# Attention in a chain of four layers: every fourth addition of exp by an adding transfer, sums in exp's own tiles, compact inversion of the softmax sums, single PSUM banks

## The chip, the cores and the metric

The kernel runs on one core of a Trainium2 chip. The metric is the device time of one execution in microseconds; the median of several runs counts. A profiled execution is one further run, of which every instruction of each engine is recorded: TensorE (PE; its weight loads are listed apart as PEld), VectorE (DVE), ScalarE (ACT), GpSimd (POOL) and the queue engine SyncE (SP), with the DMA transfers that SP, ACT and POOL issue.

## The reference

The input `x` has 16 frames of 384 channels and 16 by 16 points. Two sequences of 8 frames each make 2048 tokens. Four layers follow; the change concerns the first, attention with 12 heads of 32 channels, whose values are the input itself:

```python
xt = x.reshape(B, NUM_FRAMES, C, H, W).transpose(0, 2, 1, 3, 4)
xt = xt.reshape(B, C, N).transpose(0, 2, 1)
qk = (xt @ qk_w.T).reshape(B, N, 2, nh, HEAD_DIM)
...
v = xt.reshape(B, N, nh, HEAD_DIM).transpose(0, 2, 1, 3)
attn = jax.nn.softmax(jnp.einsum('bhnd,bhmd->bhnm', q * scale, k), axis=-1)
attn = alpha * eye + beta * attn - gamma * Cm
out = jnp.einsum('bhnm,bhmd->bhnd', attn, v)
```

`Cm` is constant (1/N). Layer 1 is a 7 by 7 depthwise convolution, a layer norm, a gelu network with a response norm and a residual; layer 2 a Sobel edge pair, a product, a layer norm and gelu; layer 3 two small products with a 3 by 3 depthwise convolution, linear attention, a layer norm and a gelu network. All is float32.

## The kernel before

**Attention** (`attention`, from L399). Channels stand on partitions, tokens along the columns; 512 tokens are a block (`BLK`), 128 a key tile. A unit is one sequence and one group of four heads (`units`, six of them); a unit has four query blocks, so 24 blocks in all, and each block has 16 steps `t`, one for each key tile: 384 steps.

A step is two halves. `scores(n, t)` makes four products `st` (one for each head, 32 channels deep, so that the four run in different rows of the PE) into two PSUM tiles of two banks each, and two exps of 1024 columns on ACT into the SBUF tiles `e`. `weighted(n, t, es)` of the step before comes after it: four products `av` (each with 32 result rows) that add e times v into one PSUM bank over all 16 steps, and the additions of `e` on DVE. The softmax needs the sum over all keys; the kernel adds the `e` of several steps on DVE into a tile `s`, and then the PE multiplies `s` with ones into the bank `dn`, which sums over partitions and spreads the sum over the 32 rows of a head. How many steps are added before such a product is in `ADDS`, one number of 16, 8, 4 or 2 for each of the 24 blocks: a small number is less adding on DVE and more products on the PE. The products of one group are put out in four quarters of 128 columns over the following steps (`weights`, through the table `due`, which holds what is to be issued at which step); a block's last group goes in one piece of 512.

At a block's end ACT copies `av` to `va`, makes `xg` (alpha times x plus the constant part), and `finish` copies `dn` to `r`. DVE inverts `r` in four pieces of 128 columns, one for each of four steps, then comes `va` times `r` and `l` (beta times that plus `xg`). ACT reads `r` once more for a bound that a check at the end looks at.

The PSUM has eight banks: three pairs for `st` (pool `pst`), one bank for `av` and one for `dn` (pool `pacc`). The q and k of later blocks are made by `project` at step 5 of a block (`SLOT`), two products at a time into one pair of banks; SP loads `v`.

PE, ACT and DVE run in the order in which the code issues (class `InOrder`). The order of everything else around attention is set by a planner: `Plan` keeps, for each engine, when it would be free, and for each pool how much room there is; each operation has a length, things it comes after, and what it takes and gives. `fill` is called in every step of attention, and `pace(t)` is its entry for the PE's and DVE's time in a step; what DVE has left goes to layer 1's convolution (`convolutions`, from step `FIRST`), which has only two `y` buffers during attention (`YB`), and from step `LEAD` to the first normalisations of layer 1 (`leads`). After attention `plan.all` orders layers 1 to 3 by the ranks in `RANK`, with `SLACK`, and `TURNS` gives the order in which blocks use the loaded weights of the two gelu networks.

Attention starts once the first x block and weights are there; the tail is almost only products of 128 by 128 by 512.

Of the kernel before, what the change touches and what calls it, by code (L numbers as in the profile page):

```python
# [13 lines left out]
PSUM = bass.MemoryType.PSUM  # L14

P = 128
# [15 lines left out]
SLOT = 5  # L32
LEAD = 20 * NQC + 6
# [3 lines left out]
    (0, ((0, 0), (0, 1), (0, 2), (0, 3),)),  # L37
    (1, ((0, 0), (0, 1),)),
    (0, ((1, 0), (1, 2),)),
    (1, ((0, 2),)),  # L40
    (0, ((1, 1), (1, 3),)),
    (1, ((1, 0), (0, 3), (1, 2), (1, 1), (1, 3),)),
# [4 lines left out]
    "mid": ((36.6, 22.0, 24.3, 85.6), (18.6, 42.9, 96.6, 26.9)),  # L47
    "l1": ((50.1, 89.5, 75.2, 4.0), (51.1, 16.8, 81.7, 28.5)),
    "l3c": ((45.7, 99.2, 100.9, 121.0), (-20.9, -6.3, 70.9, 62.0)),
    "conv": 109.4,  # L50
}
SLACK = 0.196
JUNK = 2

ADDS = (16, 8, 16, 16, 4, 4, 4, 2, 2, 8, 16, 16, 4, 16, 2, 4, 16, 8, 4, 4, 4, 4, 4, 4)
# [61 lines left out]
class Plan:  # L117
# [24 lines left out]
    def run(self, op):  # L142
        at = self.start(op)
        assert at is not None
        for tag, n in op.takes:
            del self.room[tag][:n]
        if op.engine == "PE" and at - self.free_at["PE"] > 2:
            at += 1.5
        if op.engine:
            self.free_at[op.engine] = at + op.length  # L150
        op.ready = at + op.length + op.lag
        for tag, n in op.gives:
            self.room[tag] = sorted(self.room[tag] + [op.ready] * n)
        if op.makes:
            self.made[op.makes] = op
        self.table = op.table or self.table
# [37 lines left out]
def pace(t):  # L194
# [3 lines left out]
    adds = ADDS[n]  # L198
    pe, dve = 2.066, 2.275 if t and i % adds else 0.0
    at = i - adds - 1  # L200
    parts = sum(j * adds // 4 == at % adds for j in range(4)) if at >= 0 else 0
    if parts:
        pe += 0.22 * parts
    elif i == 1 and n > 0:
        pe += 0.87
    else:
        pe += 0.09
    if n > 0:
        dve += {2: 0.88, 3: 0.88, 4: 0.88, 5: 0.88, 6: 0.6, 7: 0.66}.get(i, 0.0)
# [188 lines left out]
def attention(tc, X, xt, L0, block, small, col, cols, ones, load_qk, banks, fill, bound):  # L398
# [6 lines left out]
    with ExitStack() as actx:  # L405
# [3 lines left out]
        ep = pool("ep", 8)  # L409
        sp = pool("sp", 4)  # L410
        op = pool("op", 2)
        pst = pool("pst", 3, space=PSUM)
        pacc = pool("pacc", 1, space=PSUM)

        def bank2(name):
            return pst.tile([P, 2, BLK], F32, tag="st", name=name)

        banks.append(lambda name: bank2(name)[:, 0, :])
# [35 lines left out]
        due = {}  # L454

        def unit(u, made, gm):
# [3 lines left out]
            adds = ADDS[u * NBLK : (u + 1) * NBLK]  # L460
            acc, sums = {}, {}

            def scores(n, t):
                es = []
                for i in range(2):
                    es.append(ep.tile([P, 2, BLK], F32, tag="e", name=f"e_{u}_{n}_{t}_{i}"))
                sts = [bank2(f"st_{u}_{n}_{t}_{i}") for i in range(2)]
                for h in range(4):
                    rows = slice(HD * h, HD * (h + 1))
                    pe.matmul(  # L470
                        sts[h // 2][:, h % 2, :],
# [5 lines left out]
                for i in range(2):  # L477
                    act.activation(es[i], sts[i], AF.Exp, scale=HD**-0.5)
                return es

            def weighted(n, t, es):
                if t == 0:
                    acc["av"] = pacc.tile([P, BLK], F32, tag="av", name=f"av_{u}_{n}")
                for h in range(4):
# [3 lines left out]
                        es[h // 2][:, h % 2, :],  # L488
# [3 lines left out]
                at = t % adds[n]  # L492
                for i in range(2):
                    if at == 0:
                        sums[i] = es[i]
                    elif at == 1:
                        s = sp.tile([P, 2, BLK], F32, tag="s", name=f"s_{u}_{n}_{t}_{i}")
                        dve.tensor_tensor(s, sums[i], es[i], ALU.add)
                        sums[i] = s
                    else:  # L500
                        dve.tensor_tensor(sums[i], sums[i], es[i], ALU.add)


                k = (u * NBLK + n) * NQC + t
                if at == adds[n] - 1:
                    parts = 1 if t == NQC - 1 else 4
                    for i in range(parts):
                        due.setdefault(k + 2 + i * adds[n] // 4, []).append(
                            lambda i=i, summed=dict(sums): weights(
                                n, t, summed, ts(i, BLK // parts)  # L510
                            )
                        )
                for f in due.pop(k, ()):
                    f()
                if t == NQC - 1:
# [6 lines left out]
                    due[k + 2].append(lambda: finish(n, va, xg))  # L522

            def weights(n, t, summed, at):
                if t == adds[n] - 1 and at.start == 0:
                    acc["dn"] = pacc.tile([P, BLK], F32, tag="dn", name=f"dn_{u}_{n}")
                for h in range(4):
# [3 lines left out]
                        summed[h // 2][:, h % 2, at],  # L531
                        start=(t == adds[n] - 1 and at.start == 0),
# [3 lines left out]
            def finish(n, va, xg):  # L536
# [4 lines left out]
                r = op.tile([P, BLK], F32, tag="r", name=f"r_{u}_{n}")  # L541
                act.activation(r, acc["dn"], AF.Identity, accum_out=bound[:, 0, k : k + 1])

                def invert(i):
                    dve.reciprocal(r[:, ts(i, P)], r[:, ts(i, P)])
# [3 lines left out]

                def check():  # L550
# [1101 lines left out]
```

## Time and profile before

| what | value |
|---|---|
| runs | 2679.3 us median of 3 (2674.36 to 2680.14) |
| the profiled execution's own time | 2679.38 us |
| its span, first to last instruction | 2677.6 us |
| mean granted TensorE clock | 0.996 |
| attention, first `st` to first `ph` of layer 1 | 22.1 to 1052.3 us |
| PE busy in it | 1021.9 of 1030.2 us |
| DVE, ACT busy in it | 962.7 and 837.4 us |
| 96 reciprocals of r, 128x128 | 88.7 us, 939 ns each |
| `dn` products of 128 columns, of 512 | 84.3 us, 26.7 us |
| DMA issued by SP | 53 MB in all, mean 21 GB/s over the span |

In the profile, a group line gives the engine, the operation, `out<-in` by tile names, the form and the count, then the busy time in us, the mean of one in ns, the idle time of the engine just before, and what ended most of that idle time. L96 is the helper that issues in order, so groups are told apart by tile names. A window line gives a stretch in us, its length, then busy us and count of PE, PEld, DVE, ACT and POOL, the granted clock, the DMA share and GB/s. A timeline line gives the start in us, the length, the engine and what ran, with the idle time before it and its releaser in brackets. A DMA line gives count, size of one and median us from issue to landing.

### The profile page before, as it was taken

Reading aid. Unit: us, or ns where it says so; the run is one execution under the profiler, and the core shown is the slowest. Engines: PE = TensorE matmul, PEld = TensorE weight load, DVE = VectorE, ACT = ScalarE, POOL = GpSimd, SP = SyncE. Lnnn points to the kernel's source line nnn. Section 1 sums busy time; section 2 is a strip of 40 time slices with the busy share of each in tenths; the row PEclk is TensorE's granted clock in tenths of the full one; section 3 lists DMA queues with packets and bytes.
Section 4 is the critical chain, followed back from the end, with each engine's and each line's share of the span. In section 5 each row is a group of like instructions: output and inputs, shape, how many; then the busy total and the mean of one; then the engine's idle time right before and its main releaser. Section 6 shows DMA issues by size and latency. Waiting matters only on the chain. (4 is left out here: it accounts for less than half of the span.)

```text
span 2677.6 us, 32803 instructions
## 1 busy us (share of the span) xinstructions
PE 2644.6 (99%) x12997; PEld 1061.5 (40%) x12997; DVE 2011.5 (75%) x2588; ACT 1557.5 (58%) x2314; POOL 7.4 (0%) x54
## 2 busy tenths in 40 slices
PE   8999999999999999899999999999999999999999
PEld 2223333233323323345444454444444444454443
DVE  5999999999999889999999999999652202732300
ACT  6787878878787888564565335457443542625201
POOL 0000000000000000000000000000000000000000
PEclk9999999999999999999999999999999999999999
DMA  3000000000000003000001001011001110000000
GB/s 150 5 13 1 9 9 5 13 1 5 13 1 1 1 13 108 23 0 0 1 1 47 25 12 31 29 36 36 24 24 36 47 36 24 0 1 1 12 17 20
DMA packets 28851, 55.69 MB, mean 21 GB/s; under 512 B 1680, under 2 KB 14096, under 8 KB 28688
## 3 DMA queue, kind: packets, MB, share of 16 engines
q1 hardware_dynamic: 28544, 53.35, 6.0%
q8 instruction: 104, 1.70, 0.3%
q14 instruction: 59, 0.48, 0.1%
q10 hardware_dynamic: 144, 0.15, 0.0%
HBM read 47.21 MB, written 6.29 MB: 20 GB/s over the span
## 5 line engine op out<-in xcount | busy, mean ns | idle before, releaser
L96 ACT ACTIVATE e<-st 128x1024 f32<-128x1024 f32 x768 | 743.2, 1025 | 88.5 <-PE st L96 80.7
L96 DVE SCALAR_TENSOR_TENSOR y<-l,vec,y 128x420 f32<-128x420 f32 (+8 forms) x1152 | 660.0, 638 | 5.0
L96 DVE TENSOR_TENSOR s<-s,e 128x1024 f32<-128x1024 f32 x444 | 513.3, 1216 | 11.7 <-ACT e L96 11.2
L96 PE MATMUL st<-q,k 32*128 32x512 f32 x3072 | 474.1, 641 | 4.0 <-ACT e L96 2.3
L96 PE MATMUL av<-e,v 128*32 128x512 f32 x3072 | 410.9, 606 | 4.3 <-ACT va L96 4.2
L96 PE MATMUL ph_l<-y,wa 128*128 128x512 f32 x576 | 261.4, 597 | 0.0
L96 PE MATMUL ph_l3c<-d_l3c,wa 128*128 128x512 f32 x576 | 258.4, 593 | 0.0
L96 PE MATMUL po_l<-hid_l,wb 128*128 128x512 f32 x576 | 255.7, 596 | 1.1 <-ACT hid_l L96 1.1
L96 PE MATMUL po_l3c<-hid_l3c,wb 128*128 128x512 f32 x576 | 256.6, 593 | 0.0
L96 PEld LDWEIGHTS st<-q,k 32*128 32x128 f32 x3072 | 146.1, 183 | 220.1 <-issue 132.4
L96 DVE TENSOR_TENSOR s<-e,e 128x1024 f32<-128x1024 f32 x162 | 191.0, 1221 | 54.7 <-ACT e L96 36.0
L96 ACT ACTIVATE hid_l<-ph_l,vec 128x512 f32<-128x512 f32 x96 | 66.0, 687 | 202.9 <-PE ph_l L96 202.8
L96 ACT ACTIVATE hid_l3c<-ph_l3c,vec 128x512 f32<-128x512 f32 x96 | 65.6, 687 | 202.6 <-PE ph_l3c L96 202.5
L96 PEld LDWEIGHTS av<-e,v 128*32 128x32 f32 x3072 | 60.6, 108 | 298.1 <-issue 274.0
L96 DVE SCALAR_TENSOR_TENSOR o_l3c<-po_l3c,vec,l 128x512 f32<-128x512 f32 x24 | 17.5, 748 | 209.6 <-PE po_l3c L96 208.8
L96 PEld LDWEIGHTS po_l<-hid_l,wb 128*128 128x128 f32 x576 | 109.5, 191 | 139.1 <-issue 128.0
L96 PEld LDWEIGHTS ph_l3c<-d_l3c,wa 128*128 128x128 f32 x576 | 108.8, 190 | 137.2 <-issue 133.4
L96 PEld LDWEIGHTS ph_l<-y,wa 128*128 128x128 f32 x576 | 109.1, 191 | 136.0 <-issue 125.1
L96 PEld LDWEIGHTS po_l3c<-hid_l3c,wb 128*128 128x128 f32 x576 | 109.0, 190 | 134.6 <-issue 132.8
L96 PE MATMUL p<-x,wqk_sb 128*128 128x512 f32 x288 | 132.3, 610 | 1.2 <-DMA x<-in_x_dram 1.2
L96 DVE SCALAR_TENSOR_TENSOR g_l3a<-h_l3a,dw,g_l3a 128x450 f32<-128x450 f32 (+1 forms) x192 | 119.0, 702 | 4.2 <-ACT g_l3a L96 4.1
L96 PEld LDWEIGHTS dn<-s,ones 128*32 128x32 f32 x2016 | 64.1, 110 | 125.4 <-issue 107.0
(155 smaller groups left out, 2446.3 us busy)
## 6 DMA issues: line engine op xcount, KB each, us to landing
wa<-in_w_dram SPq DMA_DIRECT2D x9, 768.0 KB, 4.5
wb<-in_w_dram SPq DMA_DIRECT2D x9, 768.0 KB, 5.0
wa<-in_mlp_w_dram SPq DMA_DIRECT2D x9, 768.0 KB, 4.4
wb<-in_mlp_w_dram SPq DMA_DIRECT2D x9, 768.0 KB, 4.5
x<-in_x_dram SPq DMA_DIRECT2D x8, 768.0 KB, 10.6
v<-in_xt_dram SPq DMA_DIRECT2D x24, 256.0 KB, 2.7
out_dram<-o_l3c SPq DMA_DIRECT2D x24, 256.0 KB, 2.1
qkv<-in_qkv_wT_dram SPq DMA_DIRECT2D x3, 576.0 KB, 11.1
```

The source lines that it names most:

```text
L96: self.last = self.tc.keep_in_program_order(make(*args, **kw))
```

## The change

- `ADDS` goes. Every block has four groups of four steps. In a group, the second step's `e` is added to the first's by a DMA issued from POOL with `accum_op=ADD`; the fourth's is added to the third's by DVE, in place; then DVE adds the two results (`both`). The sums thus stand in `e`'s tiles, and the pool `sp` goes.
- `e` is one tile of 4 by 512 columns for a step; there are six of these where there were eight of 2 by 512 and four `s` of 2 by 512. Exp is issued for each head, 512 columns at a time.
- All eight PSUM banks are one pool of single banks, from which `st`, `av`, `dn` and the projections take.
- The quarters of `dn` come one step later; what would fall into the next block is, except for the last three blocks (`PAIRED`), collected in `late` and issued in that block's step 0, behind the projections, which move from step 5 to step 0.
- For the inversion, ACT copies `dn` to `sums`; one row of each head goes to DRAM (`away`), and comes back spread over 128 partitions of 16 columns (`few`). DVE inverts that, and it goes to DRAM (`back`) and back in four transfers that spread it over each head's 32 rows (`r`). ACT's bound reads `few`.
- `LEAD` is 24 times 16, past the last step. `pace` has new entries. The planner lets the weights' room be given back by a count of uses (`spent`). `TURNS`, `RANK` and `SLACK` have new values.

```diff
-        ep = pool("ep", 8)
-        sp = pool("sp", 4)
+        ep = pool("ep", 6)
...
-        pst = pool("pst", 3, space=PSUM)
-        pacc = pool("pacc", 1, space=PSUM)
...
+        pb = pool("pb", 8, space=PSUM, reuse_waits="tile")
+        dp = pool("dp", 2, space=DRAM)
...
-                for i in range(2):
-                    act.activation(es[i], sts[i], AF.Exp, scale=HD**-0.5)
+                for h in range(4):
+                    act.activation(es[:, h, :], sts[h], AF.Exp, scale=HD**-0.5)
...
+                if at % 2 == 0:
+                    acc[at] = es
+                elif at == 1:
+                    nc.gpsimd.dma_start(acc[0], es, accum_op=ALU.add)
+                else:
+                    dve.tensor_tensor(acc[2], acc[2], es, ALU.add)
+
+                    def both(summed=acc[0], other=acc[2]):
+                        dve.tensor_tensor(summed, summed, other, ALU.add)
+
+                    if end and block < PAIRED:
+                        late.append(both)
                     else:
...
+                        due.setdefault(k + 1, []).append(both)
+                    for i in range(1 if end else 4):
+                        f = lambda i=i, summed=acc[0]: weights(
+                            n, t, summed, ts(i, BLK if end else BLK // 4)
                         )
+                        when = k + 3 + i
+                        if block < PAIRED and when >= (block + 1) * NQC:
+                            late.append(f)
+                        else:
+                            due.setdefault(when, []).append(f)
...
-                r = op.tile([P, BLK], F32, tag="r", name=f"r_{u}_{n}")
-                act.activation(r, acc["dn"], AF.Identity, accum_out=bound[:, 0, k : k + 1])
-
-                def invert(i):
-                    dve.reciprocal(r[:, ts(i, P)], r[:, ts(i, P)])
+                sums = op.tile([P, BLK], F32, tag="sums", name=f"sums_{u}_{n}", bufs=1)
+                act.activation(sums, acc["dn"], AF.Identity, accum_out=bound[:, 0, k : k + 1])
+                away = dp.tile([4, BLK], F32, tag="away", name=f"away_{u}_{n}")
+                nc.sync.dma_start(away, sums[0:P:HD, :])
+                few = op.tile([P, BLK // HD], F32, tag="few", name=f"few_{u}_{n}")
+                nc.sync.dma_start(few, away.rearrange("h (j k) -> (h j) k", j=HD))
+                r = op.tile([P, BLK], F32, tag="r", name=f"r_{u}_{n}", bufs=1)
+
+                def invert():
+                    dve.reciprocal(few, few)
+                    back = dp.tile([P, BLK // HD], F32, tag="back", name=f"back_{u}_{n}")
+                    nc.sync.dma_start(back, few)
+                    for h in range(4):
+                        nc.sync.dma_start(
+                            r[ts(h, HD)],
+                            back[ts(h, HD)]
+                            .rearrange("j k -> (j k)")
+                            .unsqueeze(0)
+                            .to_broadcast([HD, BLK]),
+                        )
...
-                    if t == SLOT and steps:
-                        added = project(f"p_{u}_{n}", steps[:2])
-                        del steps[:2]
+                    if t == 0 and steps:
+                        fill((u * NBLK + n) * NQC, None)
+                        many = 1 if len(steps) == NBLK - 1 else 2
+                        added = project(f"p_{u}_{n}", steps[:many])
+                        del steps[:many]
+                    for f in behind:
+                        f()
+                    behind.clear()
```

The other constants:

```diff
-SLOT = 5
-LEAD = 20 * NQC + 6
+PAIRED = (NB * NC - 1) * NBLK + 1
+LEAD = 24 * NQC
...
-    pe, dve = 2.066, 2.275 if t and i % adds else 0.0
...
+    pe, dve = 2.125, 2.35 if i % 4 == 3 or i % 4 == 0 and t > 4 else 0.0
+    if 6 <= i < NQC:
+        pe += 0.16
+    if i == 0 and n > 0:
+        pe += 1.5
```

## The prediction

> **What bounds the kernel now.** I read the page's busy shares and its 40 slices first, then windows by stage, then the order of time inside attention, then the costliest groups.
>
> ```profile
> PE 2644.6 (99%) x12997; PEld 1061.5 (40%) x12997; DVE 2011.5 (75%) x2588; ACT 1557.5 (58%) x2314; POOL 7.4 (0%) x54
> PE   8999999999999999899999999999999999999999
> DVE  5999999999999889999999999999652202732300
> ...
> 22.10:1052.30 1030.20, 1021.87 (x8423) 318.42 (x8422) 962.66 (x1013) 837.38 (x992) 0.00 (x0) 1.00 0.03 8
> 1052.30:2677.60 1625.30, 1606.52 (x4545) 735.98 (x4543) 1045.59 (x1556) 716.17 (x1315) 6.74 (x48) 0.99 0.08 24
> ```
>
> TensorE is the bound in both stages: attention takes 1030.2 us of the 2677.6 us span, with PE idle for 8, and all that follows takes 1625.3, with 19 idle. DVE at 963 of 1030 looks like a second bound, but a DVE second is worth something only where PE waits for it. Inside attention the PE's steps (one of 384: four scores, four exps, four weighted sums) read like this:
>
> ```profile
> 142.23 1.14 PE L96 MATMUL st<-q,k 32*128 32x512 f32 x8
> 143.30 1.06 PE L96 MATMUL av<-e,v 128*32 128x512 f32 x8
> 143.41 4.01 ACT L96 ACTIVATE e<-st 128x1024 f32<-128x1024 f32 x4 [0.50 <-PE st L96]
> 144.30 1.31 PE L96 MATMUL st<-q,k 32*128 32x512 f32 x8
> 145.54 0.16 PEld L96 LDWEIGHTS av<-e,v 128*32 128x32 f32 x8 [0.76 <-issue]
> 145.54 1.06 PE L96 MATMUL av<-e,v 128*32 128x512 f32 x8
> 146.54 1.14 PE L96 MATMUL st<-q,k 32*128 32x512 f32 x8
> ```
>
> From one st to the next: 2.07 us, then 2.24, in turn. In the long step st takes 1.31 instead of 1.14, because half of its PSUM pair is freed late by an exp. So a plain step is 2.155 on the mean with a floor of 2.07, and the exps (four in 4.01) are not far behind.
>
> From the starts of st in the order of time I took every block's length: 41.63 where ADDS is 16 (188.2 less 146.5), 42.87 where it is 4, 45.9 where it is 2. Steps with a quarter of dn in them take 2.28, with ADDS 2 2.50; the step with two projections takes 7.42, so 5.27 above a plain one. The last four blocks hold about 10.6 us more than such sums give: layer 1's first normalisation (su, sv, square root, reciprocal) runs there. It buys a seamless hand-over:
>
> ```profile
> 1051.36 0.14 PEld L96 LDWEIGHTS dn<-s,ones 128*32 128x32 f32 x4 [0.46 <-DVE s L96]
> 1052.34 20.87 PE L96 MATMUL ph_l<-y,wa 128*128 128x512 f32 x48
> ...
> 1089.16 1.10 PE L96 MATMUL su_l<-s_l,ones 128*128 128x512 f32 x2 [3.65 <-DVE s_l L96]
> 1092.19 0.59 PE L96 MATMUL pg_l<-gs_l,ones 128*128 128x2 f32 x2 [1.93 <-DVE gs_l L96]
> ```
>
> The last exp ends at 1049.65 and ph starts 2.7 us later. Only the second block's normalisation shows, as gaps of 3.65, 1.93 and (at 1092.8) 2.13, and the granted clock is at half for 10.2 us from 1090.2 on: 5.1 us lost.
>
> **The change, part by part.**
>
> *Fewer and wider additions on DVE.*
>
> ```profile
> L96 DVE TENSOR_TENSOR s<-s,e 128x1024 f32<-128x1024 f32 x444 | 513.3, 1216 | 11.7 <-ACT e L96 11.2
> L96 DVE TENSOR_TENSOR s<-e,e 128x1024 f32<-128x1024 f32 x162 | 191.0, 1221 | 54.7 <-ACT e L96 36.0
> L96 ACT ACTIVATE e<-st 128x1024 f32<-128x1024 f32 x768 | 743.2, 1025 | 88.5 <-PE st L96 80.7
> ```
>
> 704 us go. In their place come 192 additions of 2048; 1.216 for 1024 against 0.688 for 512 (va times r) gives 1.03 ns a column, so 2.27 each, 436 in all. The 96 reciprocals (88.7) shrink to 24 of 16 columns. DVE is eased by about 355 us, but it has little to fill this with: during attention only two y buffers exist, 288 taps of layer 1's convolution, and 255 of those run there already. The other 33 at 0.64 are 21 us. On the path this part is worth 0 by itself; it lets dn come in time everywhere.
>
> *dn in four groups in every block.* Before: 81 groups (7 blocks of one, 3 of two, 11 of four, 3 of eight), now 96. They are inside the step times: ten steps of each block carry a quarter (2.28), and the block's start carries two quarters and the whole one of 512 columns: 2 times 0.21 and 1.04, so 1.46, where before the steps around the boundary cost 1.7 to 1.8, part of it av's wait for the copy of the old bank (23.2 us of weight-load waits over 23 boundaries). A second av bank removes that wait.
>
> *Single banks.* Six banks serve st as before while dn is open; in steps 0 to 5 dn isn't, and seven do. With seven only the last head waits for an exp, and that of the first head: 1.17 after st's start it begins, 0.60 later (va, 128x512, 608 ns) it is done, 1.8 in all, before the next st at 2.07. So a plain step can reach 2.07. Against it: four exps of 512. Two of 1024 start 0.922 apart; less 512 columns at 0.83 ns this gives 0.495, and va to xg shows 0.47. Four take 1.98, where two took 1.85: 4% of margin is left under 2.07. Bounds 2.07 and 2.155; I take 2.11, halfway, since both margins are thin. dn's steps leave ACT 0.3 us of air and stay at 2.28.
>
> Sum: a block is 6 times 2.11, 10 times 2.28 and 1.46, plus 5.27 for two projections; with 43 projections at 2.635 and the ramp of 0.9, the 383 steps to the last st take 997, against 1024.4 now. Attention gains 28 us (34 at 2.07, 21 at 2.155), 10.6 of them since LEAD is now past the last step and no layer 1 work runs inside.
>
> *The adding transfer.* 96 times 1 MB from POOL's queue, SBUF to SBUF, each reading both operands. Three wait for it. DVE's `both` has it late at 6.8 us. The quarters of dn follow behind that, with 8.6. Tightest is exp itself: in the changed program's order exp of step 9 takes the buffer of step 5, and that of step 13 the one of step 9. From the end of exp 5 to the start of exp 9 four steps less one run of exps pass: 9.12 less 1.98, so 7.1 us; 0.3 more is absorbed by ACT's air. No row shows such a transfer; nearest:
>
> ```profile
> wa<-in_w_dram SPq DMA_DIRECT2D x9, 768.0 KB, 4.5
> v<-in_xt_dram SPq DMA_DIRECT2D x24, 256.0 KB, 2.7
> out_dram<-o_l3c SPq DMA_DIRECT2D x24, 256.0 KB, 2.1
> ```
>
> 512 KB more cost 1.8, so 1 MB plain is 5.4; with twice the bytes read 8.9. Halfway is 7.1, just in time; I take no wait, and keep both ends: 8.9 less 7.4 is 1.5, twice a block, 72 us. The Trainium skill speaks against the change here: "DMA: Bandwidth & Descriptors", section "Measured (HBM→SBUF, 128 partitions, SWDGE, issued from GpSimd)", gives 6.15 us for a plain 1 MB without descriptor emission, and its section "SWDGE vs HWDGE vs iDMA" says that accumulating is done on that path alone. No run here shows it yet; by that figure even a plain copy fills most of the 7.1, and if the second operand doubled it, 12.3 would cost some 4.9 twice a block, about 235 us.
>
> *Sums by way of DRAM.* Seven small transfers a block on SP, in two hops out and two back. At 2.1 each a hop pair is 4.2; DVE's reciprocal stands two to three steps (4.3 to 6.5) behind the sums and va times r four steps behind that, so DVE mostly doesn't wait, and behind it only taps wait. SP's v loads stand behind these, a block ahead of their use. Hidden, 0, except after the last block, where no step covers it.
>
> *The hand-over.* Now nothing of layer 1 is ready. From the last exp on: two additions 4.7, dn 1.04, sums 0.6, two hops 4.4, reciprocal 0.2, two hops with four transfers 4.8, va and l 1.4, and only then, since DVE runs in order, s_l 1.4, su 1.0, y 1.8, squares 1.5, sums 0.7, sv 0.9, square root 0.7, reciprocal 3.35, product 1.76, affine 0.8: 31.3 where 2.7 stands now, so 28.6 more (20 if hops overlap, 34 if weight loads on SP delay them). After so long a pause I expect the half clock once: 5. Both blocks are normalised in this pause, so the 7.7 of gaps and 5.1 of clock from 1085 on go: 12.8 back. Sum 21 lost.
>
> **Sum.** 28 gained, 21 lost: 2677.6 becomes 2670.4 of span. The profiled execution's own time is 2679.38, 1.8 above its span and equal to the median of 2679.3 within 0.1, so 2672.
>
> **The rivals.**
> *The adding transfer is late (slower).* One mechanism: exp 9 and exp 13 stand on ACT until POOL's transfer lands, and st, av and the queue behind them stop. It decides from 7.4 us on, 48 us for each further microsecond. At 8.9: 2744. For it: the second operand, the figure above. Against: the 768 KB load in 4.5.
> *ACT becomes the pace (slower).* If exps of 512 don't overlap as va and xg do, four take 2.4 and every step some 2.45: 383 of these, 34 for dn at the boundaries and 113 for projections are 1086 us, 62 over now, with the hand-over's 21 2762. It decides from 2.19 a step on. Against it the 0.47 between va and xg.
> *Given back exactly.* 2.155 a step and a hand-over of 31 give 2679.
> *More gain.* 2.07 (34 gained) and a hand-over of 20 more without half clock (7 lost): 2652.
>
> **How the numbers follow.** A measurement of this kernel can't tell less than 0.2% (5.4 us) from no change. Forecast with the larger gain 0.48, within 0.2% 0.15, late transfer 0.29, ACT's pace 0.08. The forecast's own range is 2652 to 2691; taking in most of the late transfer, 2650 to 2735.
>
> **What would show it.** Plain steps of 2.07 to 2.15 and steps 9 and 13 without a wait of ACT on a DMA; adding transfers landing within 7.4 us; blocks of 42; PE idle for about 25 to 30 us before the first ph and at full clock soon after; no gaps near the second normalisation. A transfer over 7.4 us, e<-st spaced 0.6 apart, or a PE stop at block boundaries makes it wrong.

## The result and the profile after

The changed kernel takes 2778.8 us (median of 4 runs, 2775.75 to 2783.66) against 2679.2 of the kernel before in the same series: a ratio of 1.0377 (95% interval 1.0358 to 1.0397). It is 99.7 us slower, where 7 us less were forecast. The profiled execution has a span of 2776.6 us. L97 is now the helper that L96 was.

From the page of the changed kernel, the busy times and four rows of the 40 slices:

```profile
PE 2708.3 (98%) x13477; PEld 1098.3 (40%) x13477; DVE 1688.6 (61%) x2102; ACT 1590.1 (57%) x3076; POOL 90.4 (3%) x150
...
PE   9999999999999999599999999999999999999999
...
DVE  3686845876444444479999999399781364552100
...
PEclk9999999999999999799999999999999999999999
DMA  6544554545444545400011122010110010000000
```

PE is still 98% busy, and that hides the loss: in the first 16 slices it is called busy while it works slowly or stands in st for a bank. What has changed to the eye is the DMA row (0 in all but the first and the last slice of attention before, 4 to 6 now) and the hole in slice 17. Cut by stage (stretch, length, then busy time of PE, PEld, DVE, ACT, POOL, granted clock, DMA share, GB/s), with cuts at the last exp's end and at the first ph:

```profile
21.80:1116.30 1094.50, 1080.91 (x8864) 350.18 (x8864) 647.21 (x554) 870.82 (x1749) 82.93 (x96) 0.99 0.51 105
1116.30:1155.10 38.80, 10.35 (x46) 3.66 (x42) 22.11 (x20) 9.11 (x17) 0.00 (x0) 0.63 0.73 241
1155.10:2776.60 1621.50, 1601.64 (x4539) 737.58 (x4539) 1016.02 (x1510) 706.03 (x1304) 6.80 (x48) 1.00 0.08 25
```

With the same cuts the kernel before has 1027.6, 2.7 and 1625.3. So attention is 66.9 us longer, the hand-over 36.2, the rest 3.9 shorter. DVE was eased by some 315 us in attention (962.7 to 647.2), and nothing came of it.

The transfers, from the list of DMA issues (size of one, median us to landing), show the first half of the cause:

```profile
e<-e POOLq DMA_DIRECT2D x96, 1024.0 KB, 7.4
...
r<-back SPq DMA_DIRECT2D x96, 64.0 KB, 2.1
...
back<-few SPq DMA_DIRECT2D x24, 8.0 KB, 6.1
```

The adding transfer takes 6.9 us at best and 9.3 at worst. By its place in the block (groups of steps 0, 4, 8, 12) the medians are 7.05, 8.13, 7.05 and 7.16: the second one, from here on the tight one, runs beside the inversion's transfers. And 8 KB in `back` take 6.1 us. What follows from both reads like this in the order of time, at step 9 of one block:

```profile
637.57 0.86 POOL L496 DMA_DIRECT2D e<-e  x1 [7.70 <-ACT bit L97]
638.26 3.10 SPq L561 DMA_DIRECT2D r<-back  x4
...
646.10 2.07 ACT L97 ACTIVATE e<-st 128x512 f32<-128x512 f32 x4 [2.21 <-DMA e<-e]
646.41 0.69 DVE L97 TENSOR_TENSOR va<-va,r 128x512 f32<-128x512 f32 x1 [5.09 <-DMA r<-back]
647.02 1.95 DVE L97 SCALAR_TENSOR_TENSOR y<-l,vec,y 128x420 f32<-128x420 f32 x3
...
648.88 2.28 DVE L97 TENSOR_TENSOR e<-e,e 128x2048 f32<-128x2048 f32 x1
...
651.26 2.06 ACT L97 ACTIVATE e<-st 128x512 f32<-128x512 f32 x4 [3.10 <-DVE e L97]
651.75 2.29 DVE L97 TENSOR_TENSOR e<-e,e 128x2048 f32<-128x2048 f32 x1
...
651.91 2.56 PE L97 MATMUL st<-q,k 32*128 32x512 f32 x4 [1.28 <-ACT e L97]
...
654.40 1.94 PE L97 MATMUL av<-e,v 128*32 128x512 f32 x8
```

The transfer issued at 637.57 lands about 8.4 us later, so exp stands 2.21 us for it. In the same time DVE stands 5.09 us before `va` times `r`, since `r` is late behind the transfer. DVE works in order: behind `va` stand three taps of layer 1's convolution (1.95 us), so the addition that sets the next buffer free can start only at 648.88, and the next exp stands 3.10 us, for DVE this time. PE runs out of work, and its eight av then take 1.94 instead of 1.06: the granted clock is at half for 6.8 us from 652.3 on. Over attention the clock is at half for 23.9 us (6.8 before).

The mean of blocks 1 to 19, worked out from the starts of st, went from 43.01 to 46.45 us. The fastest pass of each step sums to 42.2; the mean is longer most of all at the steps around st 10, 11 and 14 (4.10, 3.18 and 2.92 us instead of 2.28).

The hand-over, with some of its instructions:

```profile
1121.37 1.06 PE L97 MATMUL dn<-e,ones 128*32 128x512 f32 x8 [3.32 <-DVE e L97]
...
1123.21 0.50 SPq L551 DMA_DIRECT2D away<-sums  x1
...
1128.78 0.25 DVE L97 RECIPROCAL few<-few 128x16 f32<-128x16 f32 x1 [7.47 <-DMA few<-away]
...
1135.90 0.69 DVE L97 TENSOR_TENSOR va<-va,r 128x512 f32<-128x512 f32 x1 [6.86 <-DMA r<-back]
...
1138.92 3.75 PE L97 MATMUL su_l<-s_l,ones 128*128 128x512 f32 x4 [16.48 <-DVE s_l L97]
...
1155.15 5.49 PE L97 MATMUL ph_l<-y,wa 128*128 128x512 f32 x6 [5.10 <-ACT y L97]
```

The last inversion goes out to DRAM and back twice with PE idle, 16.48 us before su; then comes the whole normalisation.

### The profile page after: what moved, and what is told of

Its sections match the earlier page's. It is cut to its first block, busy times and chain, and to the rows that moved or that the text cites. A ratio compares the mean times of both kernels' runs of the same rounds, so it can differ in the third digit from the quotient of the medians.

```text
span 2776.6 us, 33849 instructions
## 1 busy us (share of the span) xinstructions
PE 2708.3 (98%) x13477; PEld 1098.3 (40%) x13477; DVE 1688.6 (61%) x2102; ACT 1590.1 (57%) x3076; POOL 90.4 (3%) x150
## 5 line engine op out<-in xcount | busy, mean ns | idle before, releaser
L97 ACT ACTIVATE e<-st 128x512 f32<-128x512 f32 x1536 | 789.7, 610 | 146.8 <-PE st L97 61.3
L97 DVE SCALAR_TENSOR_TENSOR y<-l,vec,y 128x420 f32<-128x420 f32 (+8 forms) x1152 | 659.6, 641 | 10.9 <-ACT y L97 5.4
L97 DVE TENSOR_TENSOR e<-e,e 128x2048 f32<-128x2048 f32 x192 | 440.0, 2291 | 301.2 <-ACT e L97 147.7
L97 PE MATMUL st<-q,k 32*128 32x512 f32 x3072 | 505.8, 646 | 13.4 <-ACT e L97 13.1
L97 PE MATMUL av<-e,v 128*32 128x512 f32 x3072 | 428.4, 610 | 0.0
L97 PE MATMUL ph_l<-y,wa 128*128 128x512 f32 x576 | 259.8, 597 | 5.1 <-ACT y L97 5.1
L97 PE MATMUL po_l<-hid_l,wb 128*128 128x512 f32 x576 | 258.1, 597 | 3.5 <-ACT hid_l L97 3.5
L97 PE MATMUL ph_l3c<-d_l3c,wa 128*128 128x512 f32 x576 | 256.3, 593 | 0.0
L97 PE MATMUL po_l3c<-hid_l3c,wb 128*128 128x512 f32 x576 | 252.7, 593 | 0.0
L97 PEld LDWEIGHTS st<-q,k 32*128 32x128 f32 x3072 | 151.7, 184 | 226.1 <-issue 146.9
L97 ACT ACTIVATE hid_l3c<-ph_l3c,vec 128x512 f32<-128x512 f32 x96 | 65.7, 687 | 236.5 <-PE ph_l3c L97 236.3
L97 PEld LDWEIGHTS av<-e,v 128*32 128x32 f32 x3072 | 71.5, 108 | 299.4 <-issue 277.0
L97 ACT ACTIVATE hid_l<-ph_l,vec 128x512 f32<-128x512 f32 x96 | 65.6, 684 | 181.9 <-PE ph_l L97 181.4
L97 PEld LDWEIGHTS ph_l<-y,wa 128*128 128x128 f32 x576 | 110.1, 191 | 144.1 <-issue 129.7
L97 PEld LDWEIGHTS po_l<-hid_l,wb 128*128 128x128 f32 x576 | 109.4, 191 | 138.7 <-issue 125.0
L97 PEld LDWEIGHTS po_l3c<-hid_l3c,wb 128*128 128x128 f32 x576 | 109.2, 190 | 137.6 <-issue 137.1
L97 PEld LDWEIGHTS ph_l3c<-d_l3c,wa 128*128 128x128 f32 x576 | 108.8, 190 | 136.1 <-issue 134.2
L97 PEld LDWEIGHTS dn<-e,ones 128*32 128x32 f32 x2496 | 81.5, 111 | 167.3 <-issue 154.7
L97 PE MATMUL dn<-e,ones 128*32 128x128 f32 (+1 forms) x2496 | 138.4, 301 | 3.5 <-DVE e L97 3.5
L97 DVE SCALAR_TENSOR_TENSOR o_l3c<-po_l3c,vec,l 128x512 f32<-128x512 f32 x24 | 17.8, 751 | 197.2 <-PE po_l3c L97 196.1
L97 PE MATMUL p<-x,wqk_sb 128*128 128x512 f32 x288 | 131.5, 607 | 1.4 <-DMA x<-in_x_dram 1.4
L97 DVE SCALAR_TENSOR_TENSOR g_l3a<-h_l3a,dw,g_l3a 128x450 f32<-128x450 f32 (+1 forms) x192 | 119.4, 700 | 6.9 <-ACT g_l3a L97 6.8
```

The costliest lines, as they stand in the source:

```text
L97: self.last = self.tc.keep_in_program_order(make(*args, **kw))
```

## The experiments

Lengths in us; the hand-over is from the last exp's end to the first ph, the tail from there to the end. Ratios are to the kernel before, whose medians lay between 2676.9 and 2678.9 in these series. The stages are those of the profiled execution. Where an edit gives DVE other work, the planner's entry for DVE's time in a step (`pace`) is changed with it; those lines are not shown.

| kernel | time | ratio (95%) | attention | hand-over | tail |
|---|---|---|---|---|---|
| before | 2679.2 | 1 | 1027.6 | 2.7 | 1625.3 |
| changed | 2778.8 | 1.0377 (1.0358 to 1.0397) | 1094.5 | 38.9 | 1621.4 |
| e1_dve_add | 2698.1 | 1.0075 (1.0058 to 1.0092) | 1015.1 | 37.4 | 1620.7 |
| e2_old_inv | 2742.4 | 1.0237 (1.0218 to 1.0257) | 1067.7 | 29.9 | 1619.6 |
| e3_ep7 | 2753.8 | 1.0275 (1.0258 to 1.0293) | 1047.2 | 39.6 | 1643.0 |
| e4_lead | 2753.2 | 1.0282 (1.0265 to 1.0299) | 1101.1 | 7.5 | 1620.1 |
| e5_ep7_old | 2719.6 | 1.0160 (1.0144 to 1.0175) | 1024.9 | 28.8 | 1641.1 |
| e6_late_scale | 2767.0 | 1.0338 (1.0322 to 1.0354) | 1083.1 | 39.9 | 1620.5 |
| e7_dve_lead | 2682.7 | 1.0022 (1.0013 to 1.0032) | 1031.8 | 6.4 | 1625.7 |
| e8_both_lead | 2696.9 | 1.0074 (1.0060 to 1.0088) | 1026.9 | 5.7 | 1641.1 |
| e9_gate | 2681.1 | 1.0016 (1.0006 to 1.0025) | 1031.4 | 6.6 | 1620.8 |
| e10_plain | 2699.0 | one run | 1014.9 | 39.2 | 1621.8 |
| e11_eight | 2709.8 | 1.0122 (1.0106 to 1.0137) | 981.3 | 65.8 | 1637.9 |
| e12_eight_lead | 2726.9 | 1.0185 (1.0171 to 1.0199) | 994.7 | 25.2 | 1684.2 |

**e1_dve_add: the adding transfer becomes an addition on DVE.**

```diff
-                    nc.gpsimd.dma_start(acc[0], es, accum_op=ALU.add)
+                    dve.tensor_tensor(acc[0], acc[0], es, ALU.add)
```

> The adding transfer is replaced by an addition of the same 128x2048 on VectorE (2.29 us each, 96 more of them); all else is the changed kernel's. Theory A (the loss in attention is the adding transfer that lands 7.05 to 8.13 us after its issue, later than exp 9 and exp 13 need the buffer, and that holds up the small transfers of the inversion behind it): the waits of exp 9 and exp 13 for a transfer vanish, index 10 of a block goes from 4.10 to about 2.2 us, indices 11, 14 and 15 likewise, the mean block goes from 46.45 to 42.4 to 43.0 us, attention from 1094.5 to 1000 to 1015 us, the whole to 2690 to 2705 us. Theory B (the collision is with the transfers of the inversion through DRAM, whichever addition is made; VectorE stands behind them in order): VectorE still waits for r, now with 2.29 us more work in every group, and attention keeps at least half of its loss: above 1050 us, the whole above 2735. Either way the hand-over stays near 38.9 us.

Theory A holds: attention loses 79.4 us, the mean block goes to 42.88 (42.57 in most blocks), the clock is at half for 0 us of attention. In the groups of this kernel, exp's last figures are the idle time before it and what ended most of it:

```profile
L97 ACT ACTIVATE e<-st 128x512 f32<-128x512 f32 x1536 | 791.0, 609 | 66.7 <-PE st L97 63.3 <-DVE e L97 1.6
L97 DVE TENSOR_TENSOR va<-va,r 128x512 f32<-128x512 f32 x24 | 16.4, 684 | 6.3 <-DMA r<-back 6.3
L97 DVE RECIPROCAL few<-few 128x16 f32<-128x16 f32 x24 | 5.9, 246 | 7.3 <-DMA few<-away 7.3
```

The same groups in the changed kernel:

```profile
L97 ACT ACTIVATE e<-st 128x512 f32<-128x512 f32 x1536 | 789.7, 610 | 146.8 <-PE st L97 61.3 <-DMA e<-e 54.9 <-DVE e L97 23.5
L97 DVE TENSOR_TENSOR va<-va,r 128x512 f32<-128x512 f32 x24 | 16.6, 691 | 59.4 <-DMA r<-back 59.2
L97 DVE RECIPROCAL few<-few 128x16 f32<-128x16 f32 x24 | 6.0, 251 | 104.2 <-DMA few<-away 104.2
```

Of the 54.9 us for the transfer 41.0 are before exp 9 and 12.5 before exp 13. The inversion through DRAM is untouched here, and with the adding transfer gone it is hidden in every block; `back` lands in 1.4 us in the median, not 6.1. All that waiting in e1 (6.3 and 7.3) is after the last block.

**e2_old_inv: the inversion as before; the adding transfer stays.**

```diff
-                sums = op.tile([P, BLK], F32, tag="sums", name=f"sums_{u}_{n}", bufs=1)
-                act.activation(sums, acc["dn"], AF.Identity, accum_out=bound[:, 0, k : k + 1])
...
+                r = op.tile([P, BLK], F32, tag="r", name=f"r_{u}_{n}")
+                act.activation(r, acc["dn"], AF.Identity, accum_out=bound[:, 0, k : k + 1])
+                def invert(i):
+                    dve.reciprocal(r[:, ts(i, P)], r[:, ts(i, P)])
```

> The adding transfer stays; the inversion is made as in the kernel before (ACT copies dn, VectorE inverts 4 x 128 columns, no transfers through DRAM). Theory A (the adding transfer alone): group 1 lands at about 7.05 us like the others, exp 9 still waits about 0.5 to 1 us a block, the block goes from 46.45 to about 44.5 us, attention to about 1050, the hand-over loses the transfers (about 8 to 10 us of 38.9): the whole 2715 to 2735. Theory B (the transfers of the inversion are what makes the adding transfer late, and VectorE wait): nearly all waits vanish, block 42.5 to 43 us, attention 1000 to 1015, the whole 2670 to 2690. Theory C (neither; single banks and the order of the projections): no change in attention.

Nearer to A, but slower than A has it: block 45.23, attention 26.8 us shorter (1067.7, where A has about 1050), the whole 7 us above A's range and 52 above B's. The second group's transfer lands at 7.00 instead of 8.13, as both theories had it, and exp still waits for transfers:

```profile
L97 ACT ACTIVATE e<-st 128x512 f32<-128x512 f32 x1536 | 789.8, 609 | 110.3 <-PE st L97 59.5 <-DMA e<-e 39.4 <-DVE e L97 6.0
```

Against the changed kernel's own line (54.9 for the transfer, 23.5 for DVE) the wait for DVE has gone, and that for the transfer is only eased: exp 13 now stands 17.7 us for it, and the other groups' transfers land at 7.2 to 7.3 in the median and up to 9.5. v's loads, the only other transfers issued in most blocks (6.3 us each, 2.7 in the kernel before), explain few of these: of 36 landings later than 7.5 us 10 have one beside them.

**e3_ep7: a seventh buffer for exp's tiles.**

```diff
-        ep = pool("ep", 6)
+        ep = pool("ep", 7)
```

(The room comes from single `va` and `xg`, and one `s` buffer less.)

> Seven buffers for exp's tiles instead of six (paid for by one buffer less of the two temporaries of the scaling and by one of the second stage's); the transfers stay as they are. The buffer of step 5 is then asked for by exp 10 (one step, 2.1 us, later), that of step 9 by exp 14. Theory A (the transfer is late only because of the buffer): waits of exp for a transfer vanish, as 8.13 us is under 7.1 + 2.1; block from 46.45 to about 43 us, the whole 2690 to 2705. Theory B (half of the loss is VectorE waiting for r and few behind the adding transfer): block stays at 44 to 45.5 us, the whole 2720 to 2755.

Theory B: block 44.50. The waits of exp for a transfer vanish, the late landings don't (up to 9.7 us), and DVE stands before r and few as long as it did:

```profile
L97 ACT ACTIVATE e<-st 128x512 f32<-128x512 f32 x1536 | 792.0, 609 | 97.2 <-PE st L97 61.6 <-ACT e L97 18.2 <-DVE e L97 9.8
L97 DVE TENSOR_TENSOR va<-va,r 128x512 f32<-128x512 f32 x24 | 16.6, 691 | 60.5 <-DMA r<-back 55.9 <-issue 4.6
L97 DVE RECIPROCAL few<-few 128x16 f32<-128x16 f32 x24 | 6.0, 251 | 101.6 <-DMA few<-away 101.6
```

So there are two ways from one late transfer to exp: through the buffer (47.3 us here), and through what DVE has ahead of its additions. The tail, 21.6 us longer, pays for the room.

**e5_ep7_old: e2 and e3 together.**

> The adding transfer stays; seven buffers for exp's tiles and the inversion as in the kernel before, both at once (paid for by single buffers of the temporaries and one buffer of the second stage less). Alone the seventh buffer took 1.95 us off the mean block of 46.45 and the old inversion 1.22. Theory A (two separate mechanisms: exp waits for the transfer's buffer; VectorE, in order, stands before r and few, which come late behind the transfer, and the next additions and so the buffers are late): each edit removes one, together nearly all is gone: block 42.5 to 43.2 us, attention 1003 to 1018, although all 96 adding transfers still run. Theory B (one mechanism, the two edits overlap; or the transfers cost time in themselves by contention): block 44 us or more, attention above 1035. The tail is longer by about 22 us in both cases, as with the seventh buffer alone; the hand-over near 30.

Theory A for the mechanism: 69.6 us of attention are gone with all 96 adding transfers still running, where the two edits alone took 26.8 and 47.3. Block and attention are 0.15 and 7 us above A's range. Exp waits for no transfer any more, though they land no earlier (7.4 in the median):

```profile
L97 ACT ACTIVATE e<-st 128x512 f32<-128x512 f32 x1536 | 791.0, 610 | 67.0 <-PE st L97 45.3 <-ACT e L97 17.6 <-DVE e L97 0.7
```

e8 below has no adding transfer and the old inversion too. In blocks 1 to 18, ahead of the work that e8 moves into attention, its mean block is 43.08 against 43.39 here. So with the transfers running about 0.3 us a block is left; the rest was waiting.

**e6_late_scale: `va` times `r` and the sum behind it three steps later.**

```diff
-                for i, f in ((2, invert), (4, check), (6, scale), (7, put)):
+                for i, f in ((2, invert), (4, check), (9, scale), (10, put)):
```

(The planner is told so too.)

> The changed kernel with va times r and the sum behind it three steps later (steps 9 and 10 of a block instead of 6 and 7), nothing else; so VectorE reaches va about 6.5 us later, when r has mostly landed. Theory A (VectorE's stand before r, 59 us in 17 blocks, is what makes exp 10 and 11 wait; exp 9 and 13 wait for the transfer apart from it): va's wait falls under 15 us, exps' waits for VectorE vanish, the waits for the transfer stay (about 50 us); block from 46.45 to 44.8 to 45.6, the whole 2740 to 2760. Theory B (VectorE's wait for r is covered; the block loses by exp 9 and 13 alone): the whole within 8 us of 2778.8. Theory C (the wait moves to another in-order instruction, few at step 2): also no gain.

The wait falls from 59.4 to 8.2 us as expected, and the time by 11.8, where A had 19 to 39. Exp's waits for DVE fall from 23.5 to 13.2 and don't vanish, and DVE's waits partly went elsewhere: before `e` for the transfer itself 100.2 instead of 77.2. So this wait alone is worth 11.4 us of attention, where taking the inversion's transfers away altogether (e2) was worth 26.8.

**e10_plain: the second operand left out.** A plain copy in place of the adding one.

```diff
-                    nc.gpsimd.dma_start(acc[0], es, accum_op=ALU.add)
+                    nc.gpsimd.dma_start(acc[0], es)
```

> The changed kernel with the adding transfer made a plain copy of the same 1 MB, from GpSimd's queue, between the same tiles (the first step of each group is thus left out of the sum). Theory A (the second operand, read for adding, costs time): landing 5.4 to 6.2 us after the issue where it was 7.05, exp 9 and exp 13 wait less, the whole 2710 to 2750. Theory B (the transfer is bound by something else than the bytes read, its writes or its descriptors): landing 6.9 to 7.1 as before, the whole 2765 to 2790.

```profile
e<-e POOLq DMA_DIRECT2D x96, 1024.0 KB, 4.7
L97 ACT ACTIVATE e<-st 128x512 f32<-128x512 f32 x1536 | 791.2, 609 | 66.4 <-PE st L97 52.0 <-ACT e L97 11.4 <-DVE e L97 0.7
L97 DVE TENSOR_TENSOR va<-va,r 128x512 f32<-128x512 f32 x24 | 16.5, 686 | 8.4 <-DMA r<-back 8.4
L97 DVE RECIPROCAL few<-few 128x16 f32<-128x16 f32 x24 | 6.0, 250 | 111.9 <-DMA few<-away 111.9
```

Theory A, beyond its figures: 4.65 us, 6.6 at worst. With 2.4 us more air exp waits for no transfer any more, and attention is 1014.9, as if DVE did the adding. DVE still stands 111.9 us before `few`, as long as in the changed kernel: that wait costs nothing here.

**e4_lead: the first normalisations of layer 1 inside attention.**

```diff
-LEAD = 24 * NQC
+LEAD = 18 * NQC
```

> The first two normalisations of the stage after attention are made 6 blocks earlier, inside attention (their work is spread there); nothing else. The hand-over's 38.9 us, with TensorE idle 28.5 us in four pauses and then 37.5 us at half clock, is put down to the chain from the last exp through su, sv and ph. Theory A (that chain sets the hand-over): hand-over 38.9 to about 5 to 12 us, the half clock after it down to under 15 us, attention longer by what the moved work takes on TensorE (about 3 to 5 us), the whole 2735 to 2750. Theory B (the hand-over is set by the last inversion through DRAM, 4 transfers, which the next stage waits for anyway): hand-over stays above 25 us, the whole within 10 us of 2778.8.

Theory A: hand-over 7.5 us, PE idle 3.8 of it. Attention pays 6.6, where 3 to 5 had been given, and the whole is 3 us above A's range.

**e7_dve_lead: e1 and e4 together.**

> Additions on VectorE instead of the adding transfer, and the first two normalisations of the next stage inside attention; inversion through DRAM and single banks as in the changed kernel. If the two findings add up (80.7 us from the first, 25.5 from the second), 2778.8 becomes 2672.6, and since hardly any wait is left in attention for the moved work to hide in, 2668 to 2676: faster than the kernel before (2678.9) by 0.1 to 0.4%. If VectorE, with 96 additions of 2.29 us more, has no room for the moved work, attention grows by 5 to 10 us and it ends at 2678 to 2685.

The second case by the whole, 2682.7, but attention is 16.7 us longer than in e1 and not 5 to 10. (The profiled execution took 2687.4, the slowest of ten.) The price is paid in blocks 18 to 21, in step after step that is 0.3 to 0.7 us longer. sv's results lie in two of the eight PSUM banks from step 1 of block 19 to step 0 of block 20, for the square root is made only there.

**e9_gate: su and sv only in the last four steps of a block.**

```diff
-                    if op.table:
+                    if op.table or op.engine == "PE" and t % NQC < 12:
                         break
```

(with LEAD = 19 * NQC)

> As the kernel with additions on VectorE and early normalisations, but these begin one block later and their products on TensorE (su, sv) are held back to the last four steps of a block. In the kernel without this, sv took two PSUM banks in step 1 of block 19 and gave them back in step 0 of block 20, and blocks 18 to 21 were 16.6 us longer than blocks without moved work (47.1, 50.0, 43.4, 44.0 against 42.57, 40.1 for the one with a single projection). Theory A (the banks held by sv and su, of the eight that st, av and dn share, make the steps long): these blocks are 6 to 9 us longer in all (su and sv themselves are about 5), 2682.7 becomes 2672 to 2676, faster than the kernel before by 0.1 to 0.25%. Theory B (ACT's squares and VectorE's work between the exps make them long): nothing gained, 2680 to 2685.

2681.1, so the gain isn't there. sv now holds its banks only from step 12 of block 20 to step 0 of block 21, but the slow steps moved: blocks 18 to 21 take 182.8 us in all, against 184.5. The timeline shows where:

```profile
871.20 1.98 PE L97 MATMUL su_l<-s_l,ones 128*128 128x512 f32 x4
...
874.42 3.42 DVE L97 SCALAR_TENSOR_TENSOR y<-su_l,y 128x1536 f32<-128x1536 f32 x2
...
876.23 1.13 PE L97 MATMUL st<-q,k 32*128 32x512 f32 x6 [0.76 <-DVE y L97]
...
877.89 1.75 PE L97 MATMUL st<-q,k 32*128 32x512 f32 x2 [0.53 <-DVE y L97]
```

st waits for DVE to give back su's banks, and DVE had an addition of e before that. So the common pool of banks ties st to DVE as theory A says, but holding the products back doesn't loosen that tie. The kernel is 0.16% slower than the one before, which is under the 0.2% that the prediction takes for the least that can be told, and not faster.

**e8_both_lead: e7 with the old inversion.**

> As the kernel with additions on VectorE and early normalisations, and the inversion as in the kernel before (VectorE inverts 4 x 128 columns, 3.7 us a block instead of 0.25). If the inversion through DRAM does harm only behind the adding transfer, this is 0 to 6 us slower than the same with the inversion through DRAM (more work on VectorE, no less waiting): 2668 to 2680. If it does harm by itself, this is the faster of the two by 3 us or more.

2696.9, above what was given. Its attention is 4.9 us shorter than e7's, since here only one block's normalisation came inside. The tail is 15.4 longer: one pause of 12.9 us before `pd_l3a`, ended by none of the recorded work, and 5.3 before `po_l`. It doesn't tell the two inversions apart.

**e11_eight and e12_eight_lead: more additions on DVE, fewer dn products.** All additions on DVE, eight steps in a chain, in every block or in the first 18.

```diff
+                size = group(block)
+                at = t % size
+                if at == 0:
+                    acc[0] = es
                 else:
-                    dve.tensor_tensor(acc[2], acc[2], es, ALU.add)
...
+                    dve.tensor_tensor(acc[0], acc[0], es, ALU.add)
+                if at == size - 1:
```

> No adding transfer; VectorE adds the exps of eight steps one after the other into the first one's tile (14 additions a block instead of 12), so that a block needs two groups of dn products instead of four: eight quarters at 0.21 us less, 1.7 us a block, 40 us in all. Single banks, inversion through DRAM and all else as in the changed kernel. Against the kernel with four groups added on VectorE (2698.1): if VectorE, with 14 x 2.29 + 1.7 us in a block of about 41, keeps up, the block goes from 42.88 to 41.0 to 41.5, attention from 1015 to 972 to 985; about 80 of the next stage's 288 taps then come after attention, hidden behind TensorE's first products or costing up to 15: the whole 2655 to 2675, faster than the kernel before. If VectorE becomes the pace (7 additions of 2.29 in 8 steps, plus taps), attention stays above 1000 and the whole above 2680.

> The same with groups of eight in blocks 0 to 17 only, of four after them, and with the first normalisation of the next stage allowed inside attention from block 18 on (its su comes in block 22, its sv in block 23). Expected from the parts: 18 x 1.7 = 30 off the 2698.1, the hand-over from 37.4 to 8 to 15, and 5 to 15 given back for the moved work and for the second block's normalisation behind the hand-over: 2650 to 2668. If the banks that sv holds or the taps before it cost as much as the hand-over brings, it is no faster than groups of eight without it.

For attention e11 does what was worked out: 981.3 us, most blocks 41.15, and DVE keeps up. The whole, 2709.8, misses its 2655 to 2675. Only 202 of layer 1's first 288 taps are made inside; 52 of the others stand between the last exp and the first ph:

```profile
1003.20:1069.00 65.80, 10.48 (x35) 5.21 (x32) 50.70 (x72) 7.50 (x14) 0.00 (x0) 0.54 0.40 136
```

In this window DVE is busy for 50.7 of 65.8 us, PE for 10.5: what DVE doesn't do beside attention PE waits for at its end. e12, at 2726.9, misses its 2650 to 2668 by more: its hand-over is shorter (25.2), but its tail is 62.8 longer than the changed kernel's, with PE idle for 61.5 in it in many pauses; why so many stays open. No kernel tried here is faster than the one before.

## Why the prediction was wrong

**"Halfway is 7.1, just in time; I take no wait": the step that failed first.** The price of the transfer came out, 7.05 us in two of the four groups, but by luck: 7.1 was the middle between two ends, and both parts of these were off, the plain copy (5.4, measured 4.65 in e10) and the second operand (3.5, measured 2.4). What failed is the limit that the price was held against, and that the price was taken without spread. In e1, where exp waits for no transfer, steps 5 and 9 of a block read like this:

```profile
641.10 2.06 ACT L97 ACTIVATE e<-st 128x512 f32<-128x512 f32 x4 [0.18 <-PE st L97]
...
649.99 2.06 ACT L97 ACTIVATE e<-st 128x512 f32<-128x512 f32 x4 [0.22 <-PE st L97]
```

From the end of exp 5 to the start of exp 9 6.83 us pass, here and in the median of the blocks, and 7.08 from exp 9 to exp 13; the prediction had 7.1, or 7.4 with ACT's air. It had counted four steps of 2.28 less 1.98, but the steps from 5 on take 2.07, 2.19, 2.35 and 2.29, and four exps last 2.07 from the first one's start to the last one's end. In the changed kernel 0.29 us pass from the end of exp 5 to the issue. So even a transfer of 7.05 lands at 7.34, half a microsecond after exp 9 wants the buffer, and the tight group's median of 8.13 makes it 8.42. That is 1.6 us too late, 38 in 24 blocks, and exp 9 stood 41.0 us for the transfer; by the prediction's own formula, which starts at 7.4, it would have been 24. The way through the buffer cost 47.3 in all (e3). Exp 13's waits are in it, and some of the clock, which was at half for 23.9 us of attention, up to 11.9 us of work lost. The rival of the late transfer had the mechanism, and with 2744 two thirds of the loss.

**"Hidden, 0" for the sums by way of DRAM: the second step that failed.** It is true without the adding transfer (e1: no wait of DVE before the last block's end) and false beside it: `back` goes from 1.4 to 6.1 us, and DVE stands 104.2 us before few and 59.4 before va. The first of these waits is no loss by itself, for it is as long in e10, where attention loses nothing; moving the second away brought 11.4 us (e6). "Behind it only taps wait" was wrong too: the additions of e stand behind it, and exp for them. With the old inversion, which has none of these transfers, attention is 26.8 us shorter (e2), part of it because the tight group then lands earlier.

The Trainium skill, "DMA: Bandwidth & Descriptors", section "Issuing engines are not separate DMA queues", says that transfers run on the same 16 DMA engines whichever engine issued them, and interleave. The runs agree, with 1.4, 3.8 (beside plain copies, e10) and 6.1 us for the same 8 KB. The page's 6.15 us for a plain 1 MB from GpSimd's queue, which the prediction weighed, is for a load from HBM; here a plain copy between SBUF tiles took 4.65 and the adding one 7.05, so neither the 6.15 nor its double held, and the measurement decides.

**The hand-over: mis-sized.** 31.3 was the sum (its terms add up to 31.05), 38.9 the measurement. The two pairs of hops took 5.6 and 6.9 us instead of 4.4 and 4.8, 3.3 more, with the next stage's weight loads on SP between them. From l to ph 17.7 passed instead of 13.9, 3.8 more: the two blocks' normalisations are issued interleaved, so the first one waits for parts of the second, and four su took 3.75 us where they take 1.98 in e9 (the clock was at half for 27.3 us from 1123.3 on). The last 0.7 is in the additions, the sums and the scaling. "12.8 back" was wrong by 8.9: the tail is 3.9 us shorter. The gaps of the second normalisation are gone, but PE's idle time in the tail, up to its last product, is 13.2 us against 12.6 before: others came, 3.5 before the first block's `pg` and `po`, 2.7 before a `pc`.

**What was right.** A plain step takes 2.07 and 2.18 to 2.25 in turn (2.11 was the mean taken), dn's steps 2.29 (2.28), an addition of 2048 columns 2.29 (2.27). The undisturbed block is 42.57 in e1, where 42.19 had been summed; step 0, 9.07 instead of 8.84, is most of it. ACT is not the pace, and its margin is wider than thought: where nothing holds them up, exps of 512 start 0.48 us apart, so four take 1.91 of a step's 2.07 and not 1.98. So of the 28 us expected of attention 12.5 are there in e1 (1027.6 to 1015.1); the shortfall is nine or so in the block's length, and the rest in a few longer blocks.

Sum by sum: attention was to gain 28 and lost 66.9; the adding transfer and all that waited for it cost 79.4 (e1), and without it attention gains 12.5. The rest was to lose 21 and lost 32.3.

## What to carry to other kernels

Hold a transfer that must land just in time against its slowest landing beside everything else that uses the DMA engines then, not against its median alone, and add the limit up from the very steps that lie in between, not from a typical one. A late transfer comes back by several ways, and each hides the other: ask what releases the buffer, and what stands in order behind any instruction that waits for another transfer. Work moved out of a stage to ease an engine should be followed to where it then stands, for an engine that is idle in the mean can still be what the next stage waits for.

## What was not expected of the hardware

- An adding transfer of 1 MB between SBUF tiles takes 7.05 us in the median of two of the four groups, a plain copy of it 4.65: the second operand, read and added, is about 2.4 us. Its issue holds GpSimd for 0.86 us, the plain one's for 0.53.
- For 16 of the 96 adding transfers the trace has no packet of another queue between issue and landing, and each of these took 6.9 to 7.0 us (31 in e2, 6.9 to 7.03). Every one that took longer has such packets beside it: SP's, or those of the two queues that the profile's page calls "instruction". Beside the latter alone 34 took 7.45 us in the median and 9.3 at worst. That these packets make a transfer late no run here tests.
- An 8 KB transfer on SP's queue takes 1.4 us alone, 3.8 beside the plain copies and 6.1 beside the adding ones, nearly as long as the large transfer itself. Why so small a transfer waits so long no run here shows.
- In attention, leaving out step 0 of each block, 43 steps of the changed kernel took over 3 us. Five times the clock went to half in such a step, for 3.4 to 6.8 us (23.9 in all), though PE stood there for no more than 1.3 us at a time and the rest of the wait lies in its st. Other steps as long, of 5.5 us at 141.6 and 5.2 at 370.7, brought none. In e1, with four steps of 3.1 to 4.0 us, it was 0.
